# A fused adaLN, state-space and binary-weight block: the normalised input of six of eight halves is made from a channel-major copy of x instead of by transposes

## The chip, the cores and the metric

The kernel runs on one core of a Trainium2 chip, in fp32 throughout. The metric is the device time of one execution in microseconds (us); a time of a kernel is the median of several runs.

## The reference

x has 4 sequences of 512 tokens with 512 channels. A small product with a conditioning vector gives, for every sequence, shifts (sa, sb), scales (ca, cb) and gates (ga, gb). The block has two parts:

```python
h = _layernorm(x, axis=-1) * (1 + ca) + sa
x = x + ga * ssm(h, ...)                   # Mamba2-like
h = _layernorm(x, axis=-1) * (1 + cb) + sb
x = x + gb * (einsum(h, binarised weight) + bias)

# ssm(h): one projection to 3136 columns, split into xBC (2048), z (1024), A_log (64)
xBC = silu(causal_conv4(xBC) + conv_bias)  # x: 64 heads of 16; B and C: 8 groups of 64
dt = softplus(A_log)
y = chunked_scan(x, -dt, B, C, chunk=128) + D * x / dt
out = (y * silu(z + z_bias)) @ out_proj.T
```

Only the first layer norm, its scale and shift, and the product that gives A_log are touched by the change.

## The kernel before

The 2048 tokens are cut into eight **halves** of 256 tokens (two per sequence), and each half into two chunks of 128 tokens. For one half the work has a front part, the chunk work, and a tail.

The **front** of half h loads two x tiles with tokens on partitions (`load_x`), normalises them in place (`f_norm`, which calls `layer_norm`: bn_stats and bn_aggr on VectorE, variance plus epsilon, the power -0.5 on POOL, then subtract and multiply on VectorE), and turns them to channels on partitions (`f_hT`): `turned_x` makes eight transposes of 128x128 on TensorE into two PSUM tiles named phT, and ScalarE writes each of the four channel tiles of hT from PSUM while it applies the scale and shift of the sequence (tile modT). hT has 3 extra columns in front, the last three tokens of the half before, for the convolution; POOL copies them or clears them. `f_dt` then makes the step sizes: the product pa (64 columns of the projection, both chunks side by side on the output partitions), a softplus by a short series on VectorE, a running sum, and three small tensors that go to DRAM on POOL's queue (sums_d, e_d, r_d), from which SP's queue loads them again spread over partitions. `f_B`, `f_C`, `f_x` and `f_z` are the four groups of projections (pp_B, pp_C, pp_x, pp_z on TensorE) with their convolution on VectorE and tanh on ScalarE; `f_z` of j = 2 and j = 3 are the last two of a half.

The **chunk work** runs in units of 16 heads, four units for a chunk. `stage0` loads the running sums into two decay tiles of 128x1024 (SP), `stage1` takes their exponentials (ScalarE, line 549) and multiplies them with the masked B-C product (VectorE, line 625), `stage2` forms the output py from them (TensorE; py has one PSUM buffer), yt and z (VectorE and POOL) and the next state.

The **tail** of a chunk is the out projection po with the gate and the residual (`tail1`), the second layer norm and its transposes ph (`tail2`), and the binary-weight product pf (`tail3`).

The order is written out by hand as steps. The list FRONT says which front function of a half runs in which step, counted from the first step of the half before; each step also has one unit of chunk work, and eight steps make a half. So the front of half h runs beside the chunk work of half h - 1. Within this order a planner sets each engine's instruction order: it goes by the written order, but takes what is ready by its own estimate of times, and it hoists a load as soon as its buffer is free. `glued(products)` keeps a list of matmuls together behind the first of them; `tc.issue_after` puts instructions behind a given one on the same engine.

The tiles that matter here have these buffers: hT 2, x 3 (tag xa, shared with the residual tiles xr), rr 2, PSUM mm 5 (shared by phT, pa, all projections and others).

Of the kernel before, what the change touches and what calls it, by code (L numbers as in the profile page):

```python
# [11 lines left out]
F32 = mybir.dt.float32  # L12
AF = mybir.ActivationFunctionType
# [3 lines left out]
P = 128  # L17
# [23 lines left out]
def adaln_mamba_block(  # L41
    ctx: ExitStack,
    tc: tile.TileContext,
    x: bass.AP,
    w_inT: bass.AP,
    conv_w: bass.AP,
    conv_b: bass.AP,
# [23 lines left out]
    wk = ctx.enter_context(tc.tile_pool(name="wk", bufs=2))  # L71

    xs_of = {}

    def load_x(h, queue=nc.sync):
        tiles = []
        for j in range(2):
            xt = wk.tile([P, DM], F32, tag="xa", name=f"x_{h}_{j}", bufs=3)
            queue.dma_start(xt, x[h * T + j * CH : h * T + (j + 1) * CH, :])
            tiles.append(xt)  # L80
        xs_of[h] = tiles


    ct = keep.tile([P, NK, B], F32, name="ct")
# [33 lines left out]
    modT = keep.tile([P, 4, NK, B], F32, name="modT")  # L118
    gate_d = dram.tile([B, 3, DM], F32, name="gate_d")
    sums_d = dram.tile([NHALF, 2, NH, CH], F32, name="sums_d")  # L120
    e_d = dram.tile([NHALF, 2, NH, CH], F32, name="e_d")
    r_d = dram.tile([NHALF, NH, 2, CH], F32, name="r_d")

# [162 lines left out]
        nc.scalar.activation(bwT[:, :, o * P : (o + 1) * P], pt, AF.Copy, scale=2.0 / DM)  # L286


    def layer_norm(tiles, name, into=None):
        n = len(tiles)  # L290
        st = wk.tile([P, n, 6], F32, tag=f"st{n}", name=f"st_{name}")
        mv = wk.tile([P, n, 2], F32, tag=f"mv{n}", name=f"mv_{name}")
        rs = wk.tile([P, n], F32, tag=f"rs{n}", name=f"rs_{name}")
        for j, t in enumerate(tiles):
            nc.vector.bn_stats(st[:, j, :], t)
            nc.vector.bn_aggr(mv[:, j, :], st[:, j, :])
        nc.vector.tensor_scalar(rs, mv[:, :, 1], EPS, None, ALU.add)
        nc.gpsimd.tensor_tensor(rs, rs, mhalf[:, :n], ALU.pow)
        for j, t in enumerate(tiles):
            nc.vector.tensor_scalar(  # L300
                into[j], t, mv[:, j, 0:1], rs[:, j : j + 1], ALU.subtract, ALU.mult
            )


    H = [dict(B={}, C={}, xt={}, xs={}, bt={}, z={}) for _ in range(NHALF)]

    def f_norm(h):
        H[h]["xn"] = xs_of.pop(h)
        layer_norm(H[h]["xn"], f"a{h}", H[h]["xn"])

    def f_first(h):

        f_norm(h)
        for xp in xpads:
            nc.gpsimd.memset(xp, 0.0)
        for et in decays:
            nc.gpsimd.memset(et[CH // 2 :, :, 0 : CH // 2], 0.0)
        rows = first_row(1, nc.vector.tensor_copy), first_row(0, nc.scalar.copy)
        turned = [turned_x(h, d2) for d2 in range(NK // 2)]
        first_turn(1, 1, rows[0])  # L320
        first_turn(0, 0, rows[1])
        f_hT(h, turned)
        scale_small()
# [10 lines left out]

    def f_hT(h, turned=None):
        b = h // HPB

        hT = wk.tile([P, NK, KS - 1 + T], F32, tag="hT", name=f"hT_{h}")
        if h % HPB == 0:
            nc.gpsimd.memset(hT[:, :, 0 : KS - 1], 0.0)  # L340
        else:
            nc.gpsimd.tensor_copy(hT[:, :, 0 : KS - 1], H[h - 1]["hT"][:, :, T:])
        for d2 in range(NK // 2):
            pt = turned[d2] if turned else turned_x(h, d2)
            for q in range(2):
                dt = 2 * d2 + q
                nc.scalar.activation(
                    hT[:, dt, KS - 1 :], pt[:, q, :], AF.Identity,
                    bias=modT[:, 0, dt, b : b + 1], scale=modT[:, 1, dt, b : b + 1],
                )  # L350
        H[h]["hT"] = hT

    def f_dt(h):

# [8 lines left out]
            return wk.tile([P, CH], F32, tag=tag, name=f"{tag}_{h}", bufs=bufs)  # L363

        pa = ps.tile([P, CH], F32, tag="mm", name=f"pa_{h}")
        for k in range(NK):
            for c in range(2):
                mm(pa[c * NH : (c + 1) * NH, :], win[:, k, NCONV + DI :],
                   hT[:, k, KS - 1 + c * CH : KS - 1 + (c + 1) * CH], start=(k == 0), stop=(k == NK - 1))
        u, r, q, dt, relu = (small(n) for n in ("du", "dr", "dq", "da", "dl"))  # L370
        nc.vector.tensor_scalar(relu, pa, 0.0, None, ALU.max)
        nc.scalar.activation(u, pa, AF.Abs)
# [137 lines left out]
    def f_z(h, j):  # L510
        pm = ps.tile([P, 2, T], F32, tag="mm", name=f"pp_z{j}_{h}")
        for q in range(2):
            H[h]["last"] = proj(pm[:, q, :], h, NCONV + (2 * j + q) * P, KS - 1)
        u = wk.tile([P, 2, T], F32, tag="u", name=f"uz_{h}_{j}", bufs=4)
        for q in range(2):
            nc.scalar.activation(  # L516
                u[:, q, :], pm[:, q, :], AF.Identity, bias=zb[:, 2 * j + q : 2 * j + q + 1], scale=0.5
            )
        th = wk.tile([P, 2, T], F32, tag="th", name=f"thz_{h}_{j}")
        nc.scalar.activation(th, u, AF.Tanh)  # L520
        z = wk.tile([P, 2, T], F32, tag="z", name=f"z_{h}_{j}", bufs=6)
        nc.vector.scalar_tensor_tensor(z, th, 1.0, u, ALU.add, ALU.mult)
        H[h]["z"][j] = z
# [257 lines left out]
    def behind(h, f, *args):  # L781
# [3 lines left out]


    FRONT = [
        (1, load_x, ()), (2, f_norm, ()), (3, f_hT, ()), (3, f_dt, ()),
        (4, f_B, (0,)), (4, f_C, (0,)), (5, f_x, (0,)), (5, f_x, (1,)),
        (6, f_B, (1,)), (6, behind, (f_turned_sums,)), (6, f_C, (1,)), (6, behind, (f_xt, 0)),  # L790
        (7, f_x, (2,)), (7, behind, (f_xt, 1)), (7, behind, (f_Bt, 0)), (7, f_x, (3,)),
# [114 lines left out]
```

## Time and profile before

| | us |
|---|---|
| median of 3 runs | 735.48 |
| lowest and highest | 734.16 and 736.66 |
| the profiled execution, its own time | 737.38 |
| the profiled execution, its span (first to last instruction) | 735.7 |

| engine | busy us | instructions |
|---|---|---|
| TensorE, matmul (PE) | 700.4 | 5196 |
| TensorE, weight load (PEld) | 500.8 | 5196 |
| VectorE (DVE) | 599.5 | 1170 |
| ScalarE (ACT) | 522.0 | 1507 |
| GpSimd (POOL) | 254.8 | 297 |

The weight load overlaps the matmul, and ends of matmuls are modelled, so a busy PE is not PE at its peak; gaps in the weight loads are the better sign of a standing TensorE. SP only issues DMAs, on its own queue (SPq). A row of the timeline gives the start, the length, the engine, the line of the kernel, the operation, the tile written and those read, the shape, and in brackets the idle time before it with what ended it. The transposes phT of the eight halves begin at 11.6, 75.3, 179.1, 264.8, 352.5, 438.1, 525.8 and 611.4 us, so from the third half on a half takes 85.6 to 87.7 us.

### The profile page before, as it was taken

Reading aid. Unit: us, or ns where it says so; the run is one execution under the profiler, and the core shown is the slowest. Engines: PE = TensorE matmul, PEld = TensorE weight load, DVE = VectorE, ACT = ScalarE, POOL = GpSimd, SP = SyncE. Lnnn points to the kernel's source line nnn. Section 1 sums busy time; section 2 is a strip of 40 time slices with the busy share of each in tenths; the row PEclk is TensorE's granted clock in tenths of the full one; section 3 lists DMA queues with packets and bytes.
Section 4 is the critical chain, followed back from the end, with each engine's and each line's share of the span. In section 5 each row is a group of like instructions: output and inputs, shape, how many; then the busy total and the mean of one; then the engine's idle time right before and its main releaser. Section 6 shows DMA issues by size and latency. Waiting matters only on the chain.

```text
span 735.7 us, 15007 instructions
## 1 busy us (share of the span) xinstructions
PE 700.4 (95%) x5196; PEld 500.8 (68%) x5196; DVE 599.5 (81%) x1170; ACT 522.0 (71%) x1507; POOL 254.8 (35%) x297
## 2 busy tenths in 40 slices
PE   6999979899999999999999999999999999999997
PEld 3786746666677666677677666776667866677754
DVE  3869888876998678986899768996799867996995
ACT  2467658748696697785976787865968768788941
POOL 4021323444243332343223342433414332333652
PEclk9999989999999999999999999999999999999999
DMA  8991693535555256444644256552564537457720
GB/s 279 328 291 41 204 208 85 135 98 142 127 132 144 63 155 137 102 115 102 159 116 130 53 116 168 142 137 53 140 132 114 130 86 176 116 150 151 142 69 29
DMA packets 119067, 99.24 MB, mean 135 GB/s; under 512 B 73984, under 2 KB 97152, under 8 KB 118992
## 3 DMA queue, kind: packets, MB, share of 16 engines
q1 hardware_dynamic: 117808, 96.39, 52.3%
q0 software_dynamic: 896, 1.38, 0.7%
q8 instruction: 41, 0.67, 0.4%
q10 hardware_dynamic: 288, 0.52, 0.2%
q14 instruction: 34, 0.28, 0.1%
HBM read 92.47 MB, written 5.79 MB: 134 GB/s over the span
## 4 chain that ended last, share of the span: by engine, by line
PE 65%; ACT 16%; DVE 9%; DMA 4%; issue 4%; POOL 1%; SPq 1%; ACTq 0%; DVEq 0%; POOLq 0%
PE po L739 14%; PE pp_x L434 11%; PE pp_z L434 10%; ACT decay L549 9%; PE pp_C L434 7%; PE pp_B L434 5%; PE pf L775 3%; PE py L212 2%; PE py L215 2%; DVE decay L625 2%; ACT h L759 2%; DVE u_x L454 2%; DMA fw<-in_ffn_w 2%; ACT win L549 2%; PE gy L215 2%
## 5 line engine op out<-in xcount | busy, mean ns | idle before, releaser
L549 ACT ACTIVATE decay<-decay,st 128x128 f32<-128x128 f32 x960 | 293.9, 395 | 4.2 <-DMA decay<-sums_d 3.7
L625 DVE SCALAR_TENSOR_TENSOR decay<-decay,gm 128x1024 f32<-128x1024 f32 x120 | 160.8, 1341 | 50.3 <-ACT decay L549 47.2
L434 PE MATMUL pp_x<-hT,win 128*128 128x259 f32 x512 | 120.7, 390 | 7.3 <-DVE u_C L454 7.3
L434 PE MATMUL pp_z<-hT,win 128*128 128x256 f32 x512 | 118.1, 383 | 0.0
L434 PEld LDWEIGHTS pp_x<-hT,win 128*128 128x128 f32 x512 | 96.9, 193 | 25.2 <-ACT decay L549 7.7
L739 PE MATMUL po<-wout,z 128*128 128x512 f32 x256 | 113.8, 595 | 0.0
L434 PEld LDWEIGHTS pp_z<-hT,win 128*128 128x128 f32 x512 | 94.3, 189 | 16.3 <-issue 3.5
L675 POOL TENSOR_TENSOR z<-yt,z 128x256 f32<-128x256 f32 x62 | 62.9, 1015 | 76.1 <-DVE yt L674 57.8
L454 DVE SCALAR_TENSOR_TENSOR u_x<-pp_x,cw,u_x 128x256 f32<-128x256 f32 x192 | 83.6, 474 | 1.3 <-ACT u_x L450 0.7
L739 PEld LDWEIGHTS po<-wout,z 128*128 128x128 f32 x256 | 47.5, 190 | 53.1 <-issue 52.4
L672 POOL TENSOR_TENSOR yt<-yt,xs 128x256 f32<-128x256 f32 x46 | 41.4, 899 | 106.3 <-DVE yt L671 78.6
L507 POOL TENSOR_TENSOR xs<-u_x,rr 128x512 f32<-128x512 f32 x32 | 42.7, 1334 | 79.2 <-DVE u_x L459 61.3
L516 ACT ACTIVATE uz<-pp_z,zb 128x256 f32<-128x256 f32 x64 | 27.5, 470 | 59.0 <-PE pp_z L434 59.0
L215 PE MATMUL py<-decay,xpad 128*32 128x128 f32 x1680 | 66.3, 276 | 0.0
L434 PE MATMUL pp_B<-hT,win 128*128 128x259 f32 x256 | 63.5, 396 | 2.7 <-ACT decay L549 1.9
L434 PE MATMUL pp_C<-hT,win 128*128 128x259 f32 x256 | 59.6, 384 | 1.1 <-DVE u_x L454 1.1
L775 PE MATMUL pf<-bwT,h 128*128 128x512 f32 (+1 forms) x136 | 59.0, 578 | 1.4 <-ACT h L759 1.3
L434 PEld LDWEIGHTS pp_B<-hT,win 128*128 128x128 f32 x256 | 47.4, 193 | 14.5 <-ACT decay L549 3.1
L450 ACT ACTIVATE u_x<-pp_x,cb,cw 128x256 f32<-128x256 f32 x64 | 35.3, 560 | 30.5 <-PE pp_x L434 30.4
L434 PEld LDWEIGHTS pp_C<-hT,win 128*128 128x128 f32 x256 | 47.8, 189 | 9.4 <-PE pn L424 1.4
L679 POOL TENSOR_TENSOR xd<-xpad,st 128x256 f32<-128x256 f32 x48 | 34.1, 727 | 55.8 <-PE pst L215 28.3
L212 PE MATMUL py<-decay,xpad 128*32 128x128 f32 x240 | 47.4, 279 | 3.2 <-issue 2.2
(157 smaller groups left out, 1080.9 us busy)
## 6 DMA issues: line engine op xcount, KB each, us to landing
decay<-sums_d SPq DMA_DIRECT2D x120, 256.0 KB
decay<-sums_d SPq DMA_DIRECT2D x120, 128.0 KB
rr<-r_d SPq DMA_DIRECT2D x64, 128.0 KB
e<-e_d SPq DMA_DIRECT2D x96, 64.0 KB
win<-in_w_inT SPq DMA_DIRECT2D x4, 1024.0 KB
xr<-in_x SPq DMA_DIRECT2D x16, 256.0 KB
res<-o SPq DMA_DIRECT2D x15, 256.0 KB
x<-in_x SPq DMA_DIRECT2D x14, 256.0 KB
```

The costliest lines, as they stand in the source:

```text
L212: first = products[0]()
L215: product()
L434: last = mm(pm, win[:, k, col : col + P], H[h]["hT"][:, k, lo:], start=(k == 0), stop=(k == NK - 1))
L450: nc.scalar.activation(u[:, j, :], pm[:, KS - 1 :], AF.Identity, bias=cb[:, t : t + 1], scale=cw[:, t, KS - 1 : KS])
L454: nc.vector.scalar_tensor_tensor(u[:, j, :], pm[:, k : k + T], cw[:, t, k : k + 1], u[:, j, :], ALU.mult, ALU.add)
L507: nc.gpsimd.tensor_tensor(xs, xc, rr, ALU.mult)
L549: nc.scalar.activation(ets[r][:, i, :], ets[r][:, i, :], AF.Exp, bias=H[h]["st"][:, hd : hd + 1], scale=-1.0)
L625: nc.vector.scalar_tensor_tensor(ets[r], ets[r], 1.0, bc_mid(gm[:, r, :], HPG), ALU.min, ALU.mult)
L672: ew.tensor_add(t, t, xs)
L675: ew.tensor_mul(zg, t, zg)
L739: last_po = mm(po, H[h]["z"][g // 2][:, g % 2, c * CH : (c + 1) * CH], wout[:, g, :], start=(g == 0), stop=(g == NKI - 1))
L775: mm(pf, h2[:, k, :], bwT[:, k, cols], start=(k == 0), stop=(k == NK - 1))
```

## The change

From half 2 on (the third), the front gets its input twice: the x tiles as before, now only for the statistics, and a channel-major copy, which the host lays out as a second input xT (a permutation of x) and which `load_x` loads straight into hT. `f_norm` computes mean and inverse deviation per token, and POOL stores them to DRAM (stat_d, 256 tokens twice, in pieces of 4 bytes). `f_hT` loads them back broadcast to all partitions (tile mr, in the buffers of rr), subtracts and multiplies on VectorE over the whole hT in place (128x1024 each), and ScalarE applies scale and shift in place. The subtraction is made to wait for the last matmul of `f_z` 2 of the half before. `load_x` and `f_norm` stand one step earlier in FRONT. pa's products run over k from the last to the first and are glued together, in every half but the first.

```diff
@@ load_x
         xs_of[h] = tiles
+        if h > 1:
+            hT = wk.tile([P, NK, KS - 1 + T], F32, tag="hT", name=f"hT_{h}")
+            queue.dma_start(hT[:, :, KS - 1 :], xT[:, :, h * T : (h + 1) * T])
+            H[h]["hT"] = hT
@@ layer_norm: its first part is now statistics(tiles, name, rs), which returns mv
@@
     def f_norm(h):
+        if h <= 1:
+            return whole_norm(h)
+        ms = wk.tile([P, 2, 2], F32, tag="ms", name=f"ms_{h}")
+        mv = statistics(xs_of.pop(h), f"a{h}", ms[:, 1, :])
+        nc.gpsimd.tensor_copy(ms[:, 0, :], mv[:, :, 0])
+        with nc.allow_non_contiguous_dma(reason="a token's value is on its partition"):
+            nc.gpsimd.dma_start(stat_d[h].rearrange("q (j p) -> p q j", p=P), ms)
+
+    def whole_norm(h):
         H[h]["xn"] = xs_of.pop(h)
         layer_norm(H[h]["xn"], f"a{h}", H[h]["xn"])
@@ f_hT
-        hT = wk.tile([P, NK, KS - 1 + T], F32, tag="hT", name=f"hT_{h}")
+        if h <= 1:
+            if not turned:
+                turned = [turned_x(h, d2) for d2 in range(NK // 2)]
+            hT = H[h]["hT"] = wk.tile([P, NK, KS - 1 + T], F32, tag="hT", name=f"hT_{h}")
+        hT = H[h]["hT"]
...
-        for d2 in range(NK // 2):
-            pt = turned[d2] if turned else turned_x(h, d2)
-            for q in range(2):
-                dt = 2 * d2 + q
-                nc.scalar.activation(
-                    hT[:, dt, KS - 1 :], pt[:, q, :], AF.Identity,
-                    bias=modT[:, 0, dt, b : b + 1], scale=modT[:, 1, dt, b : b + 1],
-                )
-        H[h]["hT"] = hT
+        now = hT[:, :, KS - 1 :]
+        if not turned:
+            mr = wk.tile([P, 2, T], F32, tag="rr", name=f"mr_{h}")
+            nc.sync.dma_start(mr, stat_d[h].partition_broadcast(P))
+            centred = nc.vector.tensor_sub(now, now, bc_mid(mr[:, 0, :], NK))
+            tc.add_manual_dep(
+                centred.ins, H[h - 1]["z2"],
+                mybir.DependencyInfo(mybir.DependencyClass.Sync, mybir.DependencyReason.DATA),
+            )
+            nc.vector.tensor_mul(now, now, bc_mid(mr[:, 1, :], NK))
+        for dt in range(NK):
+            nc.scalar.activation(
+                now[:, dt, :], turned[dt // 2][:, dt % 2, :] if turned else now[:, dt, :], AF.Identity,
+                bias=modT[:, 0, dt, b : b + 1], scale=modT[:, 1, dt, b : b + 1],
+            )
@@ f_dt
-        for k in range(NK):
-            for c in range(2):
-                mm(pa[c * NH : (c + 1) * NH, :], win[:, k, NCONV + DI :],
-                   hT[:, k, KS - 1 + c * CH : KS - 1 + (c + 1) * CH], start=(k == 0), stop=(k == NK - 1))
+        ks = range(NK) if h == 0 else range(NK)[::-1]
+        products = [
+            partial(
+                mm, pa[c * NH : (c + 1) * NH, :], win[:, k, NCONV + DI :],
+                hT[:, k, KS - 1 + c * CH : KS - 1 + (c + 1) * CH], start=(k == ks[0]), stop=(k == ks[-1]),
+            )
+            for k in ks for c in range(2)
+        ]
+        if h == 0:
+            for product in products:
+                product()
+        else:
+            glued(products)
@@ f_z
+        H[h][f"z{j}"] = H[h]["last"].name
@@ FRONT
-        (1, load_x, ()), (2, f_norm, ()), (3, f_hT, ()), (3, f_dt, ()),
+        (0, load_x, ()), (1, f_norm, ()), (3, f_hT, ()), (3, f_dt, ()),
@@ inputs
+        "xT": cols(np.asarray(L0_attn_input_).reshape(B * L, DM).T),
```

More of the change, by code (lines that the diff above doesn't have):

```diff
@@ L44, in adaln_mamba_block @@
     x: bass.AP,
+    xT: bass.AP,
     w_inT: bass.AP,
@@ L73, in adaln_mamba_block @@
     xs_of = {}
+    H = [dict(B={}, C={}, xt={}, xs={}, bt={}, z={}) for _ in range(NHALF)]
     def load_x(h, queue=nc.sync):
@@ L120, in adaln_mamba_block @@
     sums_d = dram.tile([NHALF, 2, NH, CH], F32, name="sums_d")
+    stat_d = dram.tile([NHALF, 2, T], F32, name="stat_d")
     e_d = dram.tile([NHALF, 2, NH, CH], F32, name="e_d")
@@ L286, in turned_signs, with statistics @@
         nc.scalar.activation(bwT[:, :, o * P : (o + 1) * P], pt, AF.Copy, scale=2.0 / DM)
-    def layer_norm(tiles, name, into=None):
+    def statistics(tiles, name, rs):
         n = len(tiles)
@@ L292, in layer_norm @@
         mv = wk.tile([P, n, 2], F32, tag=f"mv{n}", name=f"mv_{name}")
-        rs = wk.tile([P, n], F32, tag=f"rs{n}", name=f"rs_{name}")
         for j, t in enumerate(tiles):
@@ L298, in layer_norm @@
         nc.gpsimd.tensor_tensor(rs, rs, mhalf[:, :n], ALU.pow)
+        return mv
+    def layer_norm(tiles, name, into=None):
+        n = len(tiles)
+        rs = wk.tile([P, n], F32, tag=f"rs{n}", name=f"rs_{name}")
+        mv = statistics(tiles, name, rs)
         for j, t in enumerate(tiles):
@@ L302, in layer_norm @@
             )
-    H = [dict(B={}, C={}, xt={}, xs={}, bt={}, z={}) for _ in range(NHALF)]
     def f_norm(h):
+        if h <= 1:
[6 more added lines that the diff above has]
+    def whole_norm(h):
         H[h]["xn"] = xs_of.pop(h)
@@ L311, in f_first @@
     def f_first(h):
-        f_norm(h)
+        whole_norm(h)
         for xp in xpads:
```

## The prediction

> **What bounds the kernel now.** I read the page's busy shares first, then cut the span at the six places where a half's transposed input begins (the tile phT), then asked for the busy time of each engine in the few microseconds behind each cut, the chain of waits through one of them, and the order of instructions there. The page and the cuts:
>
> ```profile
> PE 700.4 (95%) x5196; PEld 500.8 (68%) x5196; DVE 599.5 (81%) x1170; ACT 522.0 (71%) x1507; POOL 254.8 (35%) x297
> ```
> ```profile
> 264.78:352.52 87.74, 86.22 (x659) 62.17 (x655) 73.21 (x145) 64.65 (x187) 30.98 (x38) 1.00 0.52 125
> 352.52:438.08 85.56, 83.71 (x627) 60.56 (x623) 71.58 (x141) 64.37 (x189) 29.29 (x34) 1.00 0.49 116
> ```
>
> The columns behind the length are PE, PEld, DVE, ACT, POOL, the granted clock, DMA share, GB/s. A half takes 85.6 to 87.7 us, TensorE counts as busy for 83.7 to 86.2 of it at full clock, and every other engine has slack over a whole half (VectorE 14 us, ScalarE over 20). So over a half TensorE's queue is the limit. The seams look different:
>
> ```profile
> 263.77:270.30 6.53, 5.89 (x100) 4.13 (x100) 6.28 (x11) 6.53 (x21) 3.56 (x5) 1.00 0.55 152
> 351.51:357.50 5.99, 4.97 (x98) 3.70 (x97) 5.36 (x8) 5.96 (x18) 2.77 (x3) 1.00 0.50 147
> ```
> ```profile
> 352.34 2.43 ACT decay L549 x8
> 354.77 0.46 ACT hT L347
> 355.23 0.04 issue
> 355.27 0.44 PE pa L368 x4
> ```
>
> In the 6 us from the y product ahead of the transposes to the first B projection, ScalarE is busy without a break (6.53 of 6.53, 5.96 of 5.99) and the chain runs through its decays and hT into pa. TensorE stands still here, although it is the limit elsewhere. Its order at one seam:
>
> ```profile
> 264.78 1.09 PE L330 MATMUL phT<-ident,x 128*128 128x128 f32 x8
> 265.80 0.30 PE L212 MATMUL py<-decay,xpad 128*32 128x128 f32 x1
> 267.02 0.44 PE L368 MATMUL pa<-hT,win 128*64 128x128 f32 x4 [0.57 <-ACT hT L347]
> 268.54 0.66 PE L368 MATMUL pa<-hT,win 128*64 128x128 f32 x8
> 269.13 0.70 PE L434 MATMUL pp_B<-hT,win 128*128 128x259 f32 x2
> 269.76 0.44 PE L368 MATMUL pa<-hT,win 128*64 128x128 f32 x4
> ```
>
> Eight transposes hold the queue for 1.02 us (264.78 to 265.80), pa then waits for ScalarE's hT, and pa comes in three pieces (4, 8, 4) with other products between.
>
> **The change part by part.** It touches halves 2 to 7, six seams, and pa's order in halves 1 to 7.
>
> *Transposes.* 8 per seam go. Start to next product is 1.02 to 1.03 us at three seams. At the other three it is 1.76 to 1.90, because the next y product waits for VectorE's yt to free its only PSUM buffer (0.69 to 0.84 us idle, put down to issue; yt ends just before). There the transposes go but the wait may grow, unless the projections move ahead of it. I count 1.02 x 6 = 6.1 us. Two PSUM buffers per half come free as well; I count nothing for that.
>
> *The wait of pa for hT.* Weight loads sit idle 0.60 us (three seams) and 0.84 us (the other three) before pa, 4.3 us in all. After the change hT hangs on no transposes: it needs the load, the statistics, two VectorE operations and four on ScalarE, which may start once z2 of the half before is projected. That z2 ends at 253.1 for the seam at 264.8, some 11 us earlier. So this wait should go. What is late next is the y product behind it, which waits for decays from the same full ScalarE; I count half, 2.2 us.
>
> *pa in one piece.* Switching into or out of pa shows 0.17 to 0.34 us of idle weight loads (0.20 before its second piece, 0.17 behind it, 0.34 before its third, 0.17 behind). One piece has one entry and one exit. I take 0.35 us less at each of seven seams, 2.4 us. The reversed order of k makes its first product wait for the last tile of hT; that is no cost if hT is early.
>
> Gain together: 6.1 + 2.2 + 2.4 = 10.7 us.
>
> *VectorE.* Two tensor_scalar of 128x512 (median 546 ns) go, 1.1 us, and the 0.5 us they waited for POOL's power. Two operations with two tensors of 128x1024 come. Nearest rows: the 128x1024 scalar_tensor_tensor L625, 1.21 us undisturbed and 1.34 on the mean, or twice the 128x512 addition L743 (685 ns), 1.37. So 2.4 to 2.7 us, net +1.4 us a half. The cover is VectorE's idle time behind z2: 252.2 to 255.4 at one seam (3.2 us), 2.10 and 0.84 us idle at the next (340.6 to 344.5). Uncovered it would cost up to 2.6 x 6 = 16 us, since the decays and yt queue behind it and the y products wait for both. I charge 0.4 a half, 2.4 us.
>
> *ScalarE.* The four hT operations stay (1.91 us for four, 0.48 each) but read SBUF, not PSUM. The rows: eight 128x128 decays from SBUF take 2.44 us, 0.305 each; four h of that size from PSUM take 1.49, 0.373 each. So reading SBUF is no dearer here, and 24 operations would gain 24 x 0.068 = 1.6 us. The Trainium skill speaks against it: "Perfetto Trace Analysis", section "Optimizing Scalar/DVE Operations", gives ScalarE an access overhead of about 93 ns on SBUF and 51 ns on PSUM, which would be 24 x 0.042 = 1.0 us lost (an estimate). The h row scales by a tile as hT does and the decays by a constant, so I take neither: 0, with -1.6 and +1.0 as ends.
>
> *POOL.* The power stays (1.06 us for two columns). A copy of four numbers (the 12-column hT copy takes 0.19) and one DMA issue come. The DMA has 4-byte pieces, 512 of them; the trace has no such row. Its issues of 64 to 128 rows take 0.53 to 0.65 us, so from 0.53 to about four times 0.65 = 2.6 us if it goes by pieces; I take 1. POOL idles 6.29 us before the z product at this seam, and the issue lies a step or more ahead; 0 charged. Behind it in POOL's queue stand z and yt products which feed po; 2.6 us would fit. A gain is excluded: nothing is taken off POOL. Also, "GPSIMD Engine Reference", section "Key points", says that POOL contends with VectorE instructions that have two SBUF inputs, and both new operations do: up to 2.5 us a half of a slowed POOL, or a slowed VectorE. In the trace z takes 738 ns at the median and 1.10 us when it meets the decay product at 265.7, which itself takes 1.72 instead of 1.21. So such a meeting costs VectorE about 0.5 us; by the rule at full length I would lose 2.5 us a half of POOL time, which its idle time covers. The 0.4 above contains this.
>
> *SP and DMA.* SP gets the hT load (512 KB; nearest issue 0.46 us) and the broadcast of mean and scale (256 KB; 0.58 like rr), and the x load a step sooner. 768 KB at the 347 GB/s of the second slice of 5 us is 2.2 us of DMA time a half, beside a mean share of 0.5; the load can go as soon as the old hT is free, about 259 us for the seam at 352, where next to nothing moves. I charge 0.1 a half for late decays, 0.6 us (from 0 to 2.2 a half). The broadcast waits for the statistics to land (POOL's DMAs land in 1.8 to 1.9 us; with 4-byte pieces perhaps 4). Behind it on SP stand decay loads. The statistics are a step older, about 11 us, so I charge nothing; the first rival is the case where this fails. The broadcast also takes one of the two buffers of rr, so an rr load can wait for the multiplication; POOL has waited for rr 13.5 us in the whole run, and I add nothing.
>
> *What moves by a step.* The statistics (two bn_stats of 0.68 us, two aggregates of 0.17, one small operation of 0.22, POOL's power) go past one step's decay products and yt on VectorE and z on POOL, and two x loads of 256 KB past one step's decay loads on SP. Count and length stay. x is loaded well ahead today (VectorE waited 0.7 us for it, once), and the statistics now free the x buffers sooner, where the transposes held them a step or two longer. 0, with 1.9 us a half as the upper end if VectorE has no gap there.
>
> Sum: -10.7 + 2.4 + 0.6 = -7.7 us, against the profiled execution's 737.38 us (span 735.7 and 1.7 around it): 729.7. The median of the three timed runs is 735.48, 1.9 lower; there it makes 727.8.
>
> **The rivals.**
>
> *The broadcast comes late (slower).* SP issues in order and stood waiting 245 us for y products to free decay buffers (49 waits, mean 5, longest 15.4). If the broadcast of mean and scale stands behind such a load, VectorE blocks at its subtraction with all decays and yt behind it, and TensorE follows. It breaks even at 7.7 / 6 = 1.3 us a half; one wait of 3 us a half gives 18 - 7.7 = +10 us, 746. For it: three transfers in a row through DRAM, and a queue that is often blocked. Against it: rr takes the same way today and POOL waited for it only five times, 13.5 us in all; and the queue order follows expected readiness.
>
> *ScalarE keeps the seam (little changes).* ScalarE is full for the whole seam and the hT work is not removed. If decays slip by the 1.9 us that hT is earlier, y products wait as long as before, and only pa's pieces and a little more remain: -1.5 us, 734. For it: 6.53 of 6.53. Against it: with hT early, TensorE has 3.4 us projections to put in front.
>
> *VectorE uncovered.* 10.7 gained, 6 x 2.1 lost: 737.
>
> **How the numbers follow.** A measurement of this kernel tells about 0.3%, 2.2 us, from no change. Forecast 0.60, at 727.8, itself 722 to 732 (waits of pa and yt both gone, or half of the gain eaten). ScalarE's seam 0.16, split between faster and same. The late broadcast 0.18, slower. VectorE uncovered 0.06, a third same. Faster 0.68, same 0.10, slower 0.22. The range 722 to 740 leaves out the worse part of the late broadcast (0.12) and a larger gain (0.06); the forecast's own range is 722 to 732.
>
> **What would show it.** Right: no phT rows for halves 2 to 7; pa as one row of x16 with no wait on hT; seams of about 4.5 us; the subtraction in VectorE's gap behind z2. Wrong: VectorE rows of hT that wait for a DMA of mr, ScalarE or VectorE named before the y products for longer than now, ScalarE's hT behind decays so that pa still waits.

## The result, and the profile after

| | before | after |
|---|---|---|
| median, us | 735.23 (734.16 to 736.66, 4 runs) | 766.67 (765.81 to 769.28, 4 runs) |
| ratio, 95% interval | | 1.0433 [1.0405, 1.0461] |
| span of the profiled execution, us | 735.7 | 765.7 |
| TensorE's waits ahead of ph, py and pf, us in all | 0.4, 4.3, 1.3 | 14.6, 12.3, 6.1 |

The kernel is 31 us slower; the prediction said 727.8. (Of the runs below, two of the four of a_hold fell in a slower state of the chip and are left out of its ratio.) The page's busy row after, and two halves cut from one running sum (one operation per half on VectorE, tile dl) to the next; columns as before:

```profile
PE 700.8 (92%) x5148; PEld 501.5 (65%) x5148; DVE 609.8 (80%) x1170; ACT 522.8 (68%) x1507; POOL 268.2 (35%) x309
```
```profile
292.70:380.30 87.60, 81.36 (x636) 60.20 (x635) 71.60 (x136) 60.62 (x177) 34.14 (x40) 0.98 0.57 125
380.30:477.40 97.10, 88.81 (x627) 62.84 (x626) 77.32 (x151) 68.39 (x199) 31.59 (x36) 0.98 0.50 118
```

48 transposes are gone (5196 to 5148 matmuls), and TensorE is busy for as long as before. The granted clock in the halves fell from 1.00 to 0.98. Five halves summed, before and then after:

```profile
sum 431.40, PE 423.31 PEld 305.54 DVE 359.56 ACT 319.63 POOL 148.64; mean PE 84.66 PEld 61.11 DVE 71.91 ACT 63.93 POOL 29.73
```
```profile
sum 458.30, PE 428.95 PEld 309.24 DVE 374.94 ACT 326.13 POOL 164.91; mean PE 85.79 PEld 61.85 DVE 74.99 ACT 65.23 POOL 32.98
```

26.9 us more: 21.3 of them TensorE standing (431.4 - 423.3 = 8.1 became 458.3 - 429.0 = 29.3), 5.6 a longer busy time although 5 x 1.02 us of transposes left it. The lower clock accounts for most of this second part: 2% of 458 us is 9.2, beside 5.6 + 5.1 = 10.7.

Where TensorE stands is in the waits (engine, tile and line, who released it: us in total, times, longest):

```profile
PE ph L803 <- DVE t L316: 14.6, 7, 4.2
PE pp_x L479 <- DVE u_C L499: 6.4, 2, 5.4
PE py L222 <- DVE decay L671: 6.3, 6, 1.6
PE pf L821 <- ACT h L805: 6.1, 2, 5.5
```

The second row is nearly as long before (7.3). The others are new or grown, and only the third lies at the seam; ph and pf belong to the tail, the second layer norm and its product. First the seam, 274.98 to 280.98 us, from TensorE's timeline:

```profile
274.98 0.30 PE L222 MATMUL py<-decay,xpad 128*32 128x128 f32 x1
...
276.73 0.27 PE L222 MATMUL py<-decay,xpad 128*32 128x128 f32 x1 [0.66 <-ACT uz L562]
...
278.95 0.30 PE L222 MATMUL py<-decay,xpad 128*32 128x128 f32 x1 [1.57 <-DVE decay L671]
...
279.52 0.32 PE L222 MATMUL pa<-hT,win 128*64 128x128 f32 x1
...
280.98 3.77 PE L479 MATMUL pp_B<-hT,win 128*128 128x259 f32 x16
```

No transposes, no wait of pa, pa in one piece: all three forecast steps happened. The seam still takes 6.0 us, because the y products now wait where transposes and pa's pieces used to stand between them. At every other seam these waits are smaller (0.88 us and 0.44 to 0.68). From the end of the last pf to the start of po, the six seams take 77.6 us in all, and 78.2 before: the transposes' time is not won there, but the 31 us are lost elsewhere.

Now the tail. The chain of waits ahead of the longest standing of ph:

```profile
423.56 12.37 DMA decay<-sums_d
...
436.01 2.09 ACT decay L595 x7
...
443.76 0.61 DVE t L788
...
447.49 0.56 DVE t L316
```

A decay load issued at 423.56 landed 12.37 us later. ScalarE, VectorE and at last ph (448.18, after 4.24 us of standing) waited for it. What else was there shows in the issues on POOL's and SP's queues, and in slices of 2 us (last three columns: clock, DMA share, GB/s):

```profile
422.58 0.84 POOL L329 DMA_DIRECT2D stat_d<-ms  x1 [0.29 <-DMA decay<-sums_d]
```
```profile
423.56 0.61 SPq L588 DMA_DIRECT2D decay<-sums_d  x1
424.27 0.57 SPq L587 DMA_DIRECT2D decay<-sums_d  x1
424.89 0.59 SPq L588 DMA_DIRECT2D decay<-sums_d  x1
432.43 0.33 SPq L374 DMA_DIRECT2D mr<-stat_d  x1
```
```profile
426.00:428.00 2.00, 2.00 (x13) 1.76 (x12) 2.00 (x3) 1.45 (x5) 1.92 (x3) 1.00 0.40 11
428.00:430.00 2.00, 2.00 (x11) 1.76 (x10) 1.23 (x4) 1.04 (x2) 0.37 (x1) 1.00 0.31 18
430.00:432.00 2.00, 2.00 (x11) 1.40 (x10) 0.60 (x1) 0.00 (x0) 1.27 (x1) 1.00 0.10 12
432.00:434.00 2.00, 2.00 (x6) 0.95 (x5) 0.00 (x0) 0.00 (x0) 0.00 (x0) 1.00 0.14 37
434.00:436.00 2.00, 2.00 (x6) 0.87 (x5) 0.00 (x0) 0.00 (x0) 0.00 (x0) 1.00 0.97 247
```

The store of the statistics, 2 KB in 512 pieces of 4 bytes, was issued at 422.58. The decay loads issued just behind it moved next to nothing (11 to 18 GB/s) until it had landed at about 432, and came at 247 GB/s from 434 on. Over the six stores, from issue to landing:

```profile
DMA to landing us min/median/max: 8.6/9.7/9.8
```

POOL's other stores land in 1.8 to 1.9 us. The waits say the same for ScalarE and for SP, which issues in order and stands at the broadcast of mr:

```profile
ACT decay L595 <- DMA decay<-sums_d: 57.1, 25, 6.1
```
```profile
SPq L547 <- DMA r_d<-dr: 73.5, 9, 13.7
SPq L374 <- DMA stat_d<-ms: 42.5, 6, 9.7
```

Before, ScalarE waited for decay loads 3.7 us (4 times), and SP for r_d 3.2 us, once.

### The profile page after: what moved, and what is told of

It is laid out like the page before. It is cut to its first block, busy times and chain, and to the rows that moved or that the text cites. A ratio compares the mean times of both kernels' runs of the same rounds, so it can differ in the third digit from the quotient of the medians.

```text
span 765.7 us, 14952 instructions
## 1 busy us (share of the span) xinstructions
PE 700.8 (92%) x5148; PEld 501.5 (65%) x5148; DVE 609.8 (80%) x1170; ACT 522.8 (68%) x1507; POOL 268.2 (35%) x309
## 4 chain that ended last, share of the span: by engine, by line
PE 36%; DVE 24%; ACT 16%; DMA 15%; issue 5%; POOL 3%; SPq 1%; ACTq 0%; DVEq 0%; POOLq 0%
DMA decay<-sums_d 11%; ACT decay L595 9%; PE pp_z L479 6%; PE pp_x L479 6%; PE pf L821 5%; DVE decay L671 5%; PE po L785 4%; PE pp_C L479 3%; PE pp_B L479 3%; DVE u_x L499 2%; DVE u_C L499 2%; DVE u_B L499 2%; PE py L225 2%; ACT win L595 2%; PE py L222 2%
## 5 line engine op out<-in xcount | busy, mean ns | idle before, releaser
L671 DVE SCALAR_TENSOR_TENSOR decay<-decay,gm 128x1024 f32<-128x1024 f32 x120 | 157.6, 1315 | 70.5 <-ACT decay L595 69.1
L479 PEld LDWEIGHTS pp_z<-hT,win 128*128 128x128 f32 x512 | 94.7, 190 | 16.6 <-issue 3.4
L721 POOL TENSOR_TENSOR z<-yt,z 128x256 f32<-128x256 f32 x62 | 60.4, 974 | 101.3 <-DVE yt L720 71.3
L499 DVE SCALAR_TENSOR_TENSOR u_x<-pp_x,cw,u_x 128x256 f32<-128x256 f32 x192 | 86.7, 475 | 2.2 <-ACT u_x L495 1.3
L718 POOL TENSOR_TENSOR yt<-yt,xs 128x256 f32<-128x256 f32 x46 | 44.0, 957 | 124.6 <-DVE yt L717 68.4
L225 PE MATMUL py<-decay,xpad 128*32 128x128 f32 x1680 | 68.2, 282 | 0.0
L552 POOL TENSOR_TENSOR xs<-u_x,rr 128x512 f32<-128x512 f32 x32 | 45.4, 1420 | 62.8 <-DVE u_x L504 55.3
L821 PE MATMUL pf<-bwT,h 128*128 128x512 f32 (+1 forms) x136 | 60.8, 593 | 6.1 <-ACT h L805 6.1
L479 PE MATMUL pp_B<-hT,win 128*128 128x259 f32 x256 | 61.8, 392 | 4.7 <-DVE S L758 3.1
L222 PE MATMUL py<-decay,xpad 128*32 128x128 f32 x240 | 48.5, 285 | 10.9 <-DVE decay L671 6.3
L725 POOL TENSOR_TENSOR xd<-xpad,st 128x256 f32<-128x256 f32 x48 | 38.1, 807 | 51.0 <-ACT xpad L538 30.3
L225 PEld LDWEIGHTS py<-decay,xpad 128*32 128x32 f32 x1680 | 49.4, 112 | 0.1
```

The lines of the kernel that those rows point to most:

```text
L222: first = products[0]()
L225: product()
L479: last = mm(pm, win[:, k, col : col + P], H[h]["hT"][:, k, lo:], start=(k == 0), stop=(k == NK - 1))
L499: nc.vector.scalar_tensor_tensor(u[:, j, :], pm[:, k : k + T], cw[:, t, k : k + 1], u[:, j, :], ALU.mult, ALU.add)
L552: nc.gpsimd.tensor_tensor(xs, xc, rr, ALU.mult)
L671: nc.vector.scalar_tensor_tensor(ets[r], ets[r], 1.0, bc_mid(gm[:, r, :], HPG), ALU.min, ALU.mult)
```

## The experiments

Every run is timed against the kernel before on the same chip; its median there was 735.1 to 736.1. Kernels named a_ start from after, those named b_ from before. The three with const in their names leave the statistics out of what they compute, so only their times are of use.

### The statistics' trip

**a_const**: the broadcast reads a constant input, the store stays. **a_const_nostore**: the store goes too. **a_rows**: the four columns are turned on TensorE, so that the store is four rows of 512 bytes.

```diff
# a_const
-            nc.sync.dma_start(mr, stat_d[h].partition_broadcast(P))
+            nc.sync.dma_start(mr, <512 numbers of conv_w>.partition_broadcast(P))
# a_const_nostore: also
-            nc.gpsimd.dma_start(stat_d[h].rearrange("q (j p) -> p q j", p=P), ms)
# a_rows
-            nc.gpsimd.dma_start(stat_d[h].rearrange("q (j p) -> p q j", p=P), ms)
+        nc.tensor.transpose(pt, ms.rearrange("p q j -> p (q j)"), ident)
+        nc.scalar.copy(mst, pt)
+        nc.gpsimd.dma_start(stat_d[h].rearrange("q (j p) -> (q j) p", p=P), mst)
```

> The changed kernel, but the broadcast into mr is read from a constant input (conv_w) in place of the stored statistics, so the scaling of the input is not the reference's; the 4-byte store itself stays, and SP's order of loads is the same. Removed is only SP's wait for the store (42.5 us in six waits). Theory W (SP stands behind the store, and the decay loads behind it): most of the 31 us comes back, about 740. Theory S (the store in 512 pieces of 4 bytes holds up the decay loads that are in flight beside it): about as the changed kernel, 760 to 767. Theory O (the order on SP has turned, rr now stands ahead of decay loads and waits 73.5 us for r_d): 760 to 767 as well.

> As the run with the constant, and the 4-byte store is left out too. Same order of loads on SP. Theory S: this one falls by 15 us or more below the run with the constant, and decay loads land within 3 us. Theory W: no difference between the two, both near 740. Theory O: both stay at 755 or above, since rr still waits for r_d ahead of the decay loads.

> The changed kernel with the statistics turned on TensorE (one 128x4 transpose a half, a copy on ScalarE) and stored as four rows of 512 bytes. Theories W and S: the store lands in about 2 us in place of 9.7, SP's wait for it goes, and the time falls below 740. Theory O: rr still stands ahead of the decay loads at every seam in this kernel's order, so SP still waits for r_d some 70 us in all and the time stays above 750.

Measured: a_const 763.36 (1.0365 [1.0325, 1.0406]), a_const_nostore 751.76 (1.0216 [1.0199, 1.0232]), a_rows 781.76 (1.0618 [1.0599, 1.0637]). SP's wait for the store is worth 766.7 - 763.4 = 3.3 us (the two intervals just touch). The store itself, without anybody waiting for it, is worth 763.4 - 751.8 = 11.6. In the traces of the two, all engines go through the same instructions in the same order, the store apart, so no new order of the planner is mixed in. Without the store ScalarE's wait for decay loads falls from 53.6 to

```profile
ACT decay L593 <- DMA decay<-sums_d: 10.4, 9, 2.1
```

In a_rows the store lands in 1.6 to 3.4 us (median 2.0), and yet the kernel is 15 us slower still: the statistics now pass through TensorE and a ScalarE queue that is full, so hT itself is late: VectorE begins its subtraction 4.8 to 4.9 us behind the end of pf, where in after it begins 9.8 to 13.4 us ahead of it.

```profile
PE pa L222 <- ACT hT L386: 30.7, 7, 5.3
```

### pa alone, on the kernel before

**b_glued** puts only the new pa code (k from last to first, glued) into before. **b_rev** only reverses k. **b_gluedf** only glues. On the kernel after, **a_split** puts the old pa code back, and **a_fwd** keeps the glue but runs k forward.

```diff
# b_rev, in halves 1 to 7
-        for k in range(NK):
+        for k in range(NK)[::-1]:
# b_gluedf
+        glued(products)     # k forward, instead of the loose loop
# a_fwd
-        ks = range(NK) if h == 0 else range(NK)[::-1]
+        ks = range(NK)
```

> The kernel before, with pa's products in one piece and from the last k to the first, nothing else. My sum gave this 2.4 us: 733. If the single piece is what turns SP's order (theory O from the product alone): slower than before where the order turns, which in this kernel is two of six seams, so +3 to +10 us. If neither: 735.5 within 2 us.

> The changed kernel with pa's products as they were before (first to last k, not glued), all else changed. If the parts add: 767 less the 17 of pa, about 749. Theory O alone: the rr loads still stand ahead of decay loads at three of six seams here, so 752 to 760. If pa's piece costs only in the kernel before: 763 to 770.

> The kernel before, with pa's products over k from last to first in halves 1 to 7, but left loose (not kept together). It is the half of b_glued that does not glue. Theory P (the one piece costs: no filler is left between the y products of the seam, ScalarE sets the seam, gaps bring the half clock): pa may still be broken up, so 735 to 738. Rival V (the reversed order costs: pa's first product waits for the last tile of hT; or any edit that makes the planner order anew costs this much): 745 to 754, like b_glued's 753.5.

> The kernel before with pa's products glued, but over k from first to last as before. Theory R (the reversed order of k costs: the planner takes pa as one block behind both y products of the seam, since its first product needs hT's last tile): pa starts as early as before, 734 to 740. Rival G (the gluing costs as well: a glued list is not broken up to fill other waits): 746 to 754, like b_rev (751.2) and b_glued (753.5).

> The kernel after with pa's products over k from first to last, still glued. Theory R: most of what a_split brought (20.6) comes from the order alone: 746 to 754. Rival G: 762 to 767.

| | us | ratio, 95% interval |
|---|---|---|
| b_glued | 753.54 | 1.0235 [1.0214, 1.0257] |
| b_rev | 751.16 | 1.0219 [1.0167, 1.0271] |
| b_gluedf | 738.35 | 1.004 [1.0024, 1.0057] |
| a_split | 746.03 | 1.0146 [1.0111, 1.018] |
| a_fwd | 760.47 | 1.0338 [1.0306, 1.0369] |

On before, the new pa costs 17 us, and nearly all of it is the order of k: reversed and left loose it costs 15.5, glued and forward 2.9. The traces of b_rev and b_glued even have the same order of instructions on every engine, so the 2.4 us between these two are the spread of one program. My first theory, that the glue takes away the pieces that fill other waits, fell here: b_rev is not glued and pa still came as one row. A seam of b_rev:

```profile
356.48 1.09 PE L330 MATMUL phT<-ident,x 128*128 128x128 f32 x8
358.27 0.27 PE L212 MATMUL py<-decay,xpad 128*32 128x128 f32 x1 [0.70 <-ACT decay L549]
...
360.49 0.30 PE L212 MATMUL py<-decay,xpad 128*32 128x128 f32 x1 [1.57 <-DVE decay L625]
...
361.06 1.09 PE L368 MATMUL pa<-hT,win 128*64 128x128 f32 x16
```

With k forward, pa's first product needs only the first tile of hT and stands between the two y products, as the prediction's rows of before show it. Reversed, it needs the last tile, which ends 5.0 to 5.2 us behind the end of pf in both kernels; it comes behind both y products, and both waits lie open. In this execution the clock has no part in it: it is 1.00 in this seam and in all five halves, where TensorE stands 19.8 us (8.1 before). Of the growth, 7.5 us are ahead of the y products. Nearly as much is ahead of pp_B and pn further on, where ScalarE's h of the tail comes late (whole run; before, the second and third of these rows are 0.7 and 0.4):

```profile
PE py L212 <- DVE decay L625: 9.3, 6, 1.6
PE pp_B L434 <- ACT h L759: 6.0, 2, 3.1
PE pn L419 <- ACT h L759: 2.8, 3, 0.9
```

But it is the fastest of four executions, 747.4 us at a clock of 0.995, 11.7 above before. The others took 750.0, 752.4 and 756.7 at 0.991, 0.986 and 0.982, so a part of the 15.5 came with a lower clock.

On after the shares are others: a_split gives back 20.6 us, the order alone (a_fwd) only 6.2. There the glue costs as well. a_fwd stands longer than a_split chiefly in the tail (pf for h 14.7 us, against 7.4). Why the glue does this here and not on before, I did not find out; with another pa the planner orders all engines anew.

### SP's order

The waits of SP for r_d suggested that the loads of rr, which the planner now puts ahead of decay loads, block the queue. **b_glued_hold** and **a_hold** order rr behind the decay loads of the last unit but one of the half before.

```diff
-            nc.sync.dma_start(rr[:, r, :], ...)
+            with tc.issue_after(sums_of[h - 1, 1, 2]) if (h - 1, 1, 2) in sums_of else nullcontext():
+                nc.sync.dma_start(rr[:, r, :], ...)
```

> The kernel before with pa in one piece, and the rr loads held on SP's queue behind the decay loads of the third unit of the chunk (an order without a wait), as they stand in the kernel before at every seam. Theory O (pa's one piece costs because the planner turns SP's order at seams, so that decay loads stand behind rr and r_d): most of the 17 us comes back, 735 to 741. Rival P (the piece itself costs, by holding TensorE until the last hT tile is there, and by moving other engines' orders): stays at 748 to 754.

> The changed kernel with the rr loads held behind those decay loads on SP, nothing else. Theory O: SP's wait for r_d (73.5 us) falls below 15 us and the time falls by about 15, to 750. Theory S alone: the 4-byte store is untouched, so 762 to 768.

Measured: 748.49 (1.0164 [1.0117, 1.0212]), 5 less than b_glued but only 2.7 less than b_rev, which has the same order of instructions; and 763.27 (1.0296 [1.022, 1.0371]). The ratio of a_hold rests on two runs, 761.7 and 753.2, and puts it 1.4% or some 10 us below after. SP's wait for r_d went as intended, from 45.1 us in b_glued to 3.3 and from 73.5 to 3.5. So some 70 us less of waiting on SP's queue are worth 10 us at most by these runs, and 40 less on before are worth nothing that is clear of the spread. ScalarE's order changed along with a_hold, so even the 10 are not SP's alone.

### The trip mended

**a_rowsv_early_hold**: the row store with the copy on VectorE, the statistics another step sooner (FRONT step 0), rr held. **a_mendS**: the same row store and step, without the hold, and with pa's old loop.

```diff
-        nc.scalar.copy(mst, pt)
+        nc.vector.tensor_copy(mst, pt)
-        (0, load_x, ()), (1, f_norm, ()), (3, f_hT, ()), (3, f_dt, ()),
+        (0, load_x, ()), (0, f_norm, ()), (3, f_hT, ()), (3, f_dt, ()),
```

> The changed kernel with three mends: the statistics are turned on TensorE and stored as four rows of 512 bytes (copied from PSUM by VectorE), they stand one more step earlier, and the rr loads are held behind the decay loads on SP. Theories S, W and O together: no store that holds up decay loads, no wait of SP for it, no r_d wait ahead of decay loads, so what is left is what the change saves on TensorE: 726 to 738. If pa's piece or VectorE's two operations cost by themselves: 745 or more.

> The kernel after with three of its parts changed: statistics turned on TensorE and stored in rows of 512 B, the statistics a step sooner (step 0), pa in its old loose order. Theory P + D (piece of pa and 4-byte store make the loss): the loss of 31 falls by about 20.6 (as a_split has it) and 11.6 (as a_const_nostore has it): 735 to 740, at the level of before. Rival (something that all changed kernels share, the longer VectorE work or the broadcast, costs on its own): 745 to 750.

Measured: 748.29 (1.0168 [1.0143, 1.0194]) and 737.47 (1.0023 [1.0011, 1.0034]). With a_split these make a square:

| | store in 4-byte pieces | rows, a step sooner |
|---|---|---|
| pa reversed and glued | 766.7 (after) | 748.3 |
| pa in its old loop | 746.0 | 737.5 |

The two parts account for the loss: mending both takes 29.2 of the 31 us away. They need not add: pa's row differs by 20.6 beside the slow store and by 10.8 without it. But the upper right kernel also holds rr, which may be worth up to 10, so the right column is not clean. A second square needs neither a mend nor a hold:

| | with the statistics' trip | without store and wait |
|---|---|---|
| pa reversed and glued | 766.7 (after) | 751.8 (a_const_nostore) |
| pa in its old loop | 746.0 (a_split) | 735.3 (a_const_nostore_split, below) |

pa is worth 20.6 us with the trip and 16.5 without, the trip 14.9 and 10.8. So the two cost some 4 us more together than one by one, which the intervals hardly clear. Both parts are needed for the 31 us, and with both gone nothing is left of them.

### The clock

In a_rowsv_early_hold the granted clock fell to 0.50 for some microseconds at every seam. If too little work of TensorE in the seam were the cause, more work would be free. **a_mend_fill** adds three products of 128x512 to six seams of it.

```diff
+    def filler(n):
+        pd = ps.tile([P, DM], F32, tag="mm", name=f"pd_{n}")
+        return [partial(mm, pd, ident, wout[:, 0, :], start=True, stop=True) for _ in range(3)]
```

> a_rowsv_early_hold (748.29) with three more products of 128x512 per seam in halves 1 to 6, 18 in all, on a PSUM tile that nobody reads: work that the reference does not ask for, some 0.9 us each at full clock, 2.6 us a seam. Theory C (the half clock behind each seam is what costs, and it comes from too little TensorE activity within the seam): the added work lies where TensorE stands still, the half clock behind the seams (30.8 us in a_rowsv_early_hold) shrinks to under 12, and the time falls by up to 9 us or stays: 738 to 749. Rival (TensorE's work is simply on the path there): 18 x 0.9 = +16, 764.

Measured: 768.91 (1.0458 [1.0422, 1.0495]), 20.6 more than a_rowsv_early_hold. The added products (two matmuls each in the trace, 36) took 592 ns at full clock, 21.3 us in all, which is what the kernel lost; in the mean 682, and at worst 1222 ns, double:

```profile
L225 PE MATMUL pd<-wout,ident 128*128 128x512 f32 x36 | 19.5, 682 | 0.0
```

They came behind pa and not between the y products, where TensorE stood: the place was wrong, and the work went onto the path. That the clock can be held up by filling the gap is neither shown nor refuted; that work behind the gap costs its full length is shown.

What the clock costs shows more cleanly in one kernel against itself, below.

### ScalarE at the seam

**a_mend_dve** is a_rowsv_early_hold with hT's scale and shift on VectorE instead of ScalarE; **a_mendS_dve** is a_mendS with the same; **b_dve** does it to before; **a_mend_dve_h2** is a_mend_dve with pa loose in half 1 too.

```diff
# a_mend_dve; b_dve reads the transposes' PSUM tile instead
-            nc.scalar.activation(now[:, dt, :], now[:, dt, :], AF.Identity, bias=..., scale=...)
+            nc.vector.tensor_scalar(now[:, dt, :], now[:, dt, :], scale, bias, ALU.mult, ALU.add)
# a_mend_dve_h2
-        ks = range(NK) if h == 0 else range(NK)[::-1]
+        ks = range(NK) if h <= 1 else range(NK)[::-1]     # and loose there
```

> a_rowsv_early_hold (748.29) with hT's scale and shift of halves 2 to 7 on VectorE (one operation of 128x256 for a tile, four a half) instead of ScalarE. Theory S (ScalarE sets the seam, so that what the transposes cost comes back as waiting): 2.3 us of ScalarE per seam go, pa no longer stands behind decays, 6 x 1.5 to 2.3 = 9 to 14 us less: 734 to 740. Rival V (VectorE's queue is as full at the seam; 4 x 0.35 more there, with decays and yt behind): 748 to 756.

> The kernel before with hT's scale and shift of halves 2 to 7 on VectorE, read from the transposes' PSUM. Theory S: ScalarE's seam is shorter by 1.9 us, pa no longer waits for it: 6 x 1 to 2 less, 724 to 731. Rival (transposes still hold TensorE and VectorE has decays and yt in front of hT): 735 to 742.

> a_mendS (737.47: row store, statistics at step 0, pa loose and forward) with hT's scale and shift on VectorE. Theory S (ScalarE sets the seam): 6 x 1.5 to 2.3 us less, as the removed transposes then count too: 724 to 732. Rival (the loose pa had already filled the seam; what is left is TensorE's own work): 734 to 739, and VectorE's queue may make it slower.

> a_mend_dve (734.88) with pa loose and forward in half 1 as well as half 0, so that only halves 2 to 7, whose hT is early, have it in one piece. In a_mend_dve the first seam (half 1) takes 73.1 us between the running sums of halves 0 and 1, where before takes 65.7. Theory R (the reversed order costs where hT is late): 5 to 7 less there, of which the next half gives some back (97.4 there against 107.5 in before): 729 to 733. Rival (all of it is given back, as x and z of half 1 wait for VectorE anyway): 734 to 736.

| | us | ratio, 95% interval |
|---|---|---|
| a_mend_dve | 734.88 | 1.001 [0.9986, 1.0033] |
| b_dve | 753.43 | 1.0233 [1.0195, 1.027] |
| a_mendS_dve | 738.69 | 1.005 [1.003, 1.0069] |
| a_mend_dve_h2 | 735.87 | 0.9992 [0.9975, 1.001] |

On a_rowsv_early_hold it brings 13.4 us by the medians: pa stays reversed and glued, but hT is ready. Its last operation ends 2.9 to 3.1 us ahead of the end of pf; on ScalarE it ended 5.0 to 5.2 us behind it, though VectorE had been done for 13 us. So pa moves ahead of both remaining y products:

```profile
350.26 0.30 PE L222 MATMUL py<-decay,xpad 128*32 128x128 f32 x1
...
351.27 0.32 PE L222 MATMUL pa<-hT,win 128*64 128x128 f32 x1
...
353.63 1.14 PE L488 MATMUL pp_B<-hT,win 128*128 128x259 f32 x4
355.28 0.30 PE L222 MATMUL py<-decay,xpad 128*32 128x128 f32 x1 [0.50 <-DVE decay L683]
```

So the reversed order hurts only where hT is late; the seam from the end of pf to pp_C takes 7.4 to 8.4 us here, 9.5 to 9.7 before. b_dve is the reverse case: there hT comes off VectorE behind decays (its last operation ends 6.7 to 6.8 us behind pf), pa falls behind both y products (1.57 us for a decay before the second, as in b_rev) and the time rises by 18 us. With pa loose (a_mendS_dve) nothing is gained. a_mend_dve_h2 shows how time is handed on: from running sum to running sum, half 1's seam takes 65.0 us instead of 73.2, and the next half 104.1 instead of 97.3. No version is faster than the kernel before.

The runs of a_mend_dve lie far apart, and their time follows the granted clock: six runs at 0.995 took 731.7 to 732.8 us, seven at 0.985 to 0.986 took 739.0 to 741.4. Here 0.9% of clock goes with 8 us.

### What the removed transposes are worth

**a_const_nostore_split** is a_const_nostore with pa's old loop: the change with its trip of statistics and its pa taken away.

> The kernel after without the store of the statistics, with mean and scale read from a constant input instead (this leaves out the use of the statistics), and with pa in its old loose order. What is left of the change is the removed transposes and the two operations on VectorE. Theory L (over a half VectorE, ScalarE and POOL's small steps set the time beside TensorE, so that 5.4 us less of TensorE's work comes back as standing): 735 to 740, like a_mendS (737.5). Rival T (the statistics' trip ate the gain): 729 to 733. Sum of the earlier effects: 766.7 - 11.6 - 20.6 = 734.5.

Measured: 735.26, ratio 0.9999 [0.9989, 1.0009]. TensorE is busy for 4.4 us less than before (696.0), and the time is the same. Five halves, to be read beside the two sums above:

```profile
sum 434.10, PE 422.27 PEld 301.66 DVE 364.09 ACT 322.79 POOL 156.97; mean PE 84.45 PEld 60.33 DVE 72.82 ACT 64.56 POOL 31.39
```

TensorE stands 11.8 us in them, 8.1 before. Where the transposes' time went shows in the seams by themselves, on TensorE's timeline, from the end of the last pf to the start of po; all have the same products there, but for the transposes (and some of a chunk's small products at the first seam of a_mendS_dve):

| | the six seams, us | in all | last hT ends, from the end of pf |
|---|---|---|---|
| before | 13.2, 13.0, 13.0, 13.0, 13.0, 13.0 | 78.2 | +5.0 to +5.2 |
| after | 12.1, 13.1, 12.1, 13.0, 14.2, 13.1 | 77.6 | +2.5 to +4.1 |
| a_const_nostore | 16.7, 14.8, 16.6, 14.8, 13.9, 15.4 | 92.3 | +5.0 to +5.2 |
| a_const_nostore_split | 11.9, 13.0, 11.8, 13.0, 11.8, 13.0 | 74.4 | +5.0 to +5.2 |
| a_mendS_dve | 11.8, 11.0, 11.8, 11.0, 11.8, 11.0 | 68.2 | -1.4 to -3.0 |

In a_const_nostore_split three seams are 1.2 us shorter and three are not: there a y product now waits 0.90 us ("issue") and pa still 0.66 for hT, which ends as late as before because its four operations sit in ScalarE's queue. With these on VectorE (a_mendS_dve) all six are shorter, by 10 us in all; so ScalarE did hold the seam. Yet neither kernel is faster than before: the halves lose most of what their seams win. In a_mendS_dve TensorE stands longer behind the seam, where it stood 0.7 and 0.4 us before:

```profile
PE pp_B L479 <- ACT h L805: 3.4, 3, 1.2
PE pn L464 <- ACT h L805: 3.3, 2, 1.7
```

That the transposes' removal brings no time is shown. What sets the pace over a whole half is not: VectorE has more work in both (603.7 and 622.3 us, 599.5 before), as theory L has it, and no run takes that away by itself.

The pair a_const_nostore and its split also places pa's cost: 17.9 us more at the seams, 16.5 in all.

## Why the prediction was wrong, step by step

*Transposes, -6.1.* They went, and brought nothing: 735.26 in a_const_nostore_split, against 735.83 beside it. The failed step is to count their 1.02 us a seam as time on the path, since "over a half TensorE's queue is the limit". At three seams 1.2 us were won and mostly lost again later in the half; at the other three nothing was. These were the seams of 1.02 to 1.03, which the step took for safe; those where "the wait may grow" were the ones that shrank. The rival "ScalarE keeps the seam" had the outcome (it said -1.5), and hT on VectorE shows that ScalarE did hold the seam; but relieving it brought no time either (it put more work on VectorE), so it is not the whole cause. Which engine sets the half stays open.

*pa's wait, -2.2.* At the six seams it left (1.6 us are at half 1, whose input is still transposed), and the y product behind it took over, as named; not half of the gain was eaten but all of it: 6.3 us for decays on VectorE and 4.7 for ScalarE (four rows of waits) at the six seams.

*pa in one piece, -2.4.* The failed step with the largest cost: +16.5 us without the statistics' trip, 20.6 with it; on before 15.5 for the order and 2.9 for the glue alone. The step said that reversed k "is no cost if hT is early". The condition was right, as a_mend_dve shows, but hT was not early. VectorE was done with it 6 to 11 us ahead of the end of pf, but ScalarE's four operations kept their place behind its decays, and the last ended 2.5 to 4.1 us behind it. And the pieces of pa, priced as switching cost, were what kept TensorE at work between y products.

*VectorE, +2.4.* The subtraction took 1.22 to 1.95 us and the product 1.22 to 2.19 (predicted 2.4 to 2.7 for both); VectorE's total rose by 10.3 us, 1.7 a half against 1.4. Sized about right. In five of six halves they did not sit in a gap behind z2 but right behind other work (t at 447.95), and once VectorE stood ahead of them (5.5 us, put down to mr). What they cost in time, no run shows by itself.

*ScalarE, 0.* Here row and rule disagreed, and the rule was right. hT from PSUM in halves 0 and 1 and from SBUF in the others:

```profile
L383 ACT ACTIVATE hT<-hT,modT 128x256 f32<-128x256 f32 x24 | 13.1, 604 | 0.0
L383 ACT ACTIVATE hT<-phT,modT 128x256 f32<-128x256 f32 x8 | 3.9, 564 | 2.6 <-DVE cb L217 1.8 <-PE phT L355 0.7
```

0.040 us each more, 24 x 0.040 = 1.0 us, the upper end taken from the Trainium skill ("Perfetto Trace Analysis", "Optimizing Scalar/DVE Operations"). The decay and h rows were of other forms and gave the wrong sign.

*POOL, 0.* The issue took 0.84 us where I had taken 1: right.

*SP and DMA, +0.6, and the landing "perhaps 4".* This is the other failed term that makes the loss: 9.7 us landing, and 11.6 us of time for the store by a_const against a_const_nostore, 2 a half instead of 0.1. The trace of before had no store of 4-byte pieces, and the "perhaps 4" had nothing of its kind behind it. The page I had not weighed speaks of it: the Trainium skill, "DMA: Bandwidth & Descriptors", "Rules for kernel authors", says that a non-contiguous last dimension becomes one descriptor per element, and its "Specifications" put the least size for full rate at 512 bytes. The landing in rows of 512 bytes (2.0 us) agrees. That such a store holds up loads on another queue stands in neither row nor rule that I used; the slices at 426 to 434 us show it, and a_const_nostore that the store is the cause.

*The late broadcast.* Right about the place (SP, decay loads behind it) and the sign, wrong about the means: SP's own wait made 3.3 us. That its 746 equals a_split's 746.0, the change without its pa part, is chance.

Step by step, then, the 31 us: SP's wait about 3.3, the store 11.6, pa's order and glue 16.5 (with what the planner made of them), and the change without these three takes 735.26, the time of before. The clock, at 0.98, is contained in each of these and not a part of its own.

## What to carry to other kernels

Before counting removed work as a gain, ask what sets the whole period and not only the stretch: here seams that were 4 to 10 us shorter in all brought no time. A matmul group that can start on partial input is a filler; its order of k decides where it can stand, so write it to start with what is ready first. Price a store by its pieces, and by what stands behind it in the DMA engines, not by its bytes.

## What the runs showed of the hardware

A store of 2 KB in 512 pieces of 4 bytes took 8.6 to 9.8 us to land, in rows of 512 bytes 1.6 to 2.0 at the median; while the first was under way, loads of 128 and 256 KB issued behind it on another queue moved at 11 to 18 GB/s and landed in up to 12.4 us. Single packets of the loads were drawn out: of 8192 packets of 4 KB, which take 0.2 us at the median, 109 took over 1 us in after (92 of them begun during one of the six stores, the longest 6.3 us), 96 in a_const and 1 in a_const_nostore. What holds them the trace does not show.

TensorE's granted clock falls to half behind standing much shorter than I expected to matter. After 1.67 us of it, which ended at 221.8 in the kernel after (clock and DMA columns last):

```profile
223.00:225.00 2.00, 2.00 (x6) 1.59 (x5) 2.00 (x6) 2.00 (x7) 0.00 (x0) 0.50 0.85 188
```

and behind ph's 4.24 us:

```profile
448.00:450.00 2.00, 1.82 (x20) 1.46 (x24) 1.97 (x3) 2.00 (x8) 1.88 (x1) 0.53 0.02 4
450.00:452.00 2.00, 2.00 (x33) 1.38 (x26) 1.74 (x3) 1.50 (x5) 0.43 (x2) 0.62 0.06 25
```

The Trainium skill ("TensorE: Matmul & The Clock Gate", "HAM oscillation") warns of idle gaps over about 3.4 us. The second case agrees; the first is half that gap. And it is no fixed price: b_rev stands 1.5 to 1.6 us ahead of one y product at each seam and keeps 1.00 in its profiled execution, while three others of the same kernel had 0.982 to 0.991.

The twenty traces together show more of the rule. Their stretches at half clock last 3.41 us, or two or three times that, and all changes of the clock in a trace lie on one grid of 3.41 us. Of 87 falls, 84 followed a cell of this grid in which TensorE was busy for 1.76 us or less, about half of it (the other three lie in the first 30 us; the ends of matmuls are modelled, so a tenth of a us means little). No cell at full clock with less than 1.41 us was followed by full clock; between 1.41 and 1.76 both occur. The cell ahead of the fall at 222.8 had 1.68 us. In b_rev every cell from 110 to 740 us had 1.70 or more. So where a wait lies against the grid helps to decide whether it costs clock. That this is why executions of one kernel differ is a guess: their other traces are not kept.
